# Every fifth chunk of layer 1's weighting goes from DVE to ACT

## The chip, the cores and the metric

The kernel runs on one core of a Trainium2 chip. The time is device microseconds of the whole kernel. Beside the unprofiled runs there is one profiled execution, with a trace of every instruction; its own time and its span (first to last instruction in the trace) are given below. Engines are called PE (matmul), DVE (vector), ACT (scalar), POOL (GpSimd, which issues the gathers) and SP (which issues the plain DMAs).

## The reference, cut to what matters

Two graph-attention layers on 2048 nodes with 256 features, 8 batches, one sparse adjacency shared by all (the probability of an edge is 2 x 0.0039, and every node is its own neighbour). Each layer is followed by a residual and a layer norm. Layer 1, where the change is:

```python
q = (h @ W).reshape(B, N, H, D)                 # H = 4 heads, D = 64
e_src = jnp.einsum('bnhd,d->bnh', q, a_src)
e_dst = jnp.einsum('bnhd,d->bnh', q, a_dst)
e = e_src[:, :, None, :] + e_dst[:, None, :, :]
e = jnp.where(e >= 0, e, 0.2 * e)
e = jnp.where(mask, e, NEG_INF)                 # mask: the adjacency
attn = jax.nn.softmax(e, axis=2)
h_prime = jnp.einsum('bijh,bjhd->bihd', attn, q)
y = layernorm(x + elu(h_prime))
```

Only neighbours count: for node i, head h and batch b the kernel sums attn x q over the 12 to 38 neighbours of i and no others.

## The kernel before, in words

**Tiling.** The nodes are sorted by degree and cut into 16 tiles of 128. Tile t has room for K = `SLOTS[t]` neighbours (38, 24, 23, 21, 20, 19, 19, 18, 17, 17, 16, 15, 15, 14, 13, 12). The batches are taken in two halves of four. One unit of work is (layer, half h, tile t), so each layer has 32 units. In layer 1 the tiles of half 0 run from t = 15 down to 8, then 0, then 7 to 1; those of half 1 in the reverse of that order, so the last unit of all is t = 15 with K = 12.

**A unit of layer 1.** POOL gathers, slot by slot, the k-th neighbour's row of 128 nodes with an indirect DMA (L189: 128 rows, each with 4 batches of 256 features and 4 logit terms). Two slots make a chunk (`CHUNK`), which fills one tile of a ring of 16 (`RING`); a chunk's ring tile is free again when PE has summed it. K = 38 is done in two parts of 19 slots, all others in one.

- `logits1`: DVE adds the node's own term to each chunk's logit terms (L744, one per chunk), then leaky ReLU, mask and softmax over the K slots (L752 to L759, exp on ACT at L760, sum and reciprocal L766 and L768). `pw = p / sum` goes into a PSUM tile (L769); `p` itself stays in SBUF, without the division. For K = 38 `pw` is the copy of `p` without division (L771), and the two parts are combined later.
- `sums1`: per chunk DVE multiplies the rows in place by `pw`, one weight for each slot, batch, head and its 64 columns (L793, 2048 columns for two slots, 1024 for the last chunk of an odd K). PE then adds each slot into PSUM by products with the identity (L609, four of 64x64 per slot, into two `acc` tiles per part; there are four such tiles in all).
- `after1`: for K = 38 the two parts are scaled and added (`shares`, L813, L819). Then ELU and residual (ACT L824, L825 give `ex`; DVE L829, L832), statistics (DVE L370, L371), `z` (ACT L381, L382), `rstd` and `nmr` (DVE L383 to L389), normalising on ACT (L393), and four scatters of the result by POOL (L197).

**What sets the order.** A generator scheduler written in the kernel (`tick`) emits the instructions: the sums of one unit are interleaved with the logits of the units ahead and the `after1` of the unit before. POOL's queue runs in exactly that order (`manual_schedule` for Pool). The instructions of the other engines are placed by the framework's own scheduler, so their order in the built program isn't always the emitted one. Credits on the ring (`pump`) let a gather be emitted only when a tile is due to come free.

In layer 0 the logits are dot products on DVE (L540), and the weighting there is done on ACT already, 256 columns at a time (L631).

Of the kernel before, what the change touches and what calls it, by code (L numbers as in the profile page):

```python
# [16 lines left out]
AF = mybir.ActivationFunctionType  # L17
ALU = mybir.AluOpType
# [4 lines left out]
P = 128  # L23
ALPHA = 0.2
EPS = 1e-5
H = 4
D = 64
# [10 lines left out]
CHUNK = 2  # L38
RING = 16
LEAD = 5  # L40
LATE = 6

FAR = float(2**16)

# [79 lines left out]
def fast_path(  # L124
# [24 lines left out]
    nc = tc.nc  # L149
# [3 lines left out]
    HB = B // 2  # L153
    HC = HB * C
    HG = HB * H
# [19 lines left out]
    def ps_tile(name):  # L175
        return ps.tile([P, 512], F32, tag="ps", name=name)

    def acc_tile(name):
        return psa.tile([P, 512], F32, tag="acc", name=name)
# [66 lines left out]
    for it in range(NT):  # L246
        v = adjs[it][:, :N]
# [30 lines left out]
    for it in range(NT):  # L278
# [6 lines left out]
        i = it // 2  # L285
# [138 lines left out]
    class Unit:  # L424
        def __init__(self, layer, h, t):
            self.layer, self.h, self.t = layer, h, t
            self.K = SLOTS[t]
            self.name = f"{layer}_{h}_{t}"

            n = self.K if self.K <= RING * CHUNK * 3 // 4 else -(-self.K // 2)  # L430
            self.parts = [(k, min(n, self.K - k)) for k in range(0, self.K, n)]
            self.chunks = [[] for _ in self.parts]
            self.p = [None] * len(self.parts)

            self.m, self.s = [], []
            self.ready = False
# [166 lines left out]
    def add_slot(u, acc, k, K, rows, s):  # L603

        w_ = (C, CD)[u.layer]
        for c in range(2):
            for r in range(2):
                rr = slice(64 * r, 64 * r + 64)
                nc.tensor.matmul(  # L609
                    acc[r][64 * c : 64 * c + 64, :],  # L610
                    lhsT=ident[rr, rr],
                    rhs=rows[rr, s, c * 2 * w_ : (c + 1) * 2 * w_].rearrange(
                        "p (j w) -> p j w", j=2
                    )[:, :, :C],
                    start=(k == 0),
                    stop=(k == K - 1),
                    tile_position=(64 * r, 64 * c),
                )
# [110 lines left out]
    def logits1(u):  # L729

        while not u.ready:
            yield 0
        for i, (k0, K) in enumerate(u.parts):
            n, o = f"{u.name}_{i}", offs[u.t] + k0
            wide = [P, K, HG]
            so = u.own.rearrange("p (b g) -> p b g", b=HB)
            e = ep.tile(wide, F32, tag="e", name=f"e_{n}")
            for c in range(-(-K // CHUNK)):
                while len(u.chunks[i]) <= c:
                    yield 0  # L740
                while clock[0] < u.chunks[i][c][2] + 5:
                    yield 0
                rows, ns, _ = u.chunks[i][c]
                nc.vector.tensor_tensor(  # L744
                    e[:, c * CHUNK : c * CHUNK + ns, :].rearrange("p s (b g) -> p s b g", b=HB),
                    rows[:, :ns, :].rearrange("p s (b w) -> p s b w", b=HB)[:, :, :, C:],
                    so.unsqueeze(1).to_broadcast([P, ns, HB, H]),
                    ALU.add,
                )
                yield ns  # L750
            p = e
            nc.vector.scalar_tensor_tensor(p, e, ALPHA, e, ALU.mult, ALU.max)  # L752
            nc.vector.tensor_tensor(
                p, p, neg[:, o : o + K].unsqueeze(2).to_broadcast(wide), ALU.add
            )
            yield 0
            m = sp.tile([P, HG], F32, tag="m1", name=f"m1_{n}")
            nc.vector.tensor_reduce(m, p.rearrange("p k c -> p c k"), AX.X, ALU.max)
            nc.vector.tensor_tensor(p, p, m.unsqueeze(1).to_broadcast(wide), ALU.subtract)  # L759
            nc.scalar.activation(p, p, AF.Exp)  # L760
            yield 0
            yield 0

            pw = ps_tile(f"p_{n}")[:, : K * HG].rearrange("p (k c) -> p k c", k=K)
            sm = sp.tile([P, HG], F32, tag="s1", name=f"s1_{n}")
            nc.vector.tensor_reduce(sm, p.rearrange("p k c -> p c k"), AX.X, ALU.add)  # L766
            if len(u.parts) == 1:
                nc.vector.reciprocal(sm, sm)  # L768
                nc.vector.tensor_tensor(pw, p, sm.unsqueeze(1).to_broadcast(wide), ALU.mult)  # L769
            else:  # L770
                nc.vector.tensor_copy(pw, p)  # L771
            u.m.append(m)
            u.s.append(sm)
            u.p[i] = pw
            yield 0

    def sums1(u):
        u.xr = xrp.tile([P, 2, HW], F32, tag="xr", name=f"xr_{u.name}")
        nc.sync.dma_start(u.xr.rearrange("p r c -> p (r c)"), x1s[u.h][ts(u.t, P), :])
        while evictions:  # L780
            evictions.popleft()()
        u.accs = []
        for i, (k0, K) in enumerate(u.parts):
            while u.p[i] is None:
                yield 0
            acc = [acc_tile(f"acc_{u.name}_{i}_{r}") for r in range(2)]
            for c in range(-(-K // CHUNK)):
                rows, n, _ = u.chunks[i][c]
                v = rows[:, :n, :].rearrange("p s (b w) -> p (s b) w", b=HB)
                v = v[:, :, :C].rearrange("p a (g d) -> p a g d", d=D)  # L790
                pv = u.p[i][:, c * CHUNK : c * CHUNK + n, :]
                pv = pv.rearrange("p k (b g) -> p (k b) g", b=HB)
                nc.vector.tensor_tensor(  # L793
                    v, v, pv.unsqueeze(3).to_broadcast([P, n * HB, H, D]), ALU.mult
                )
                for s in range(n):
                    add_slot(u, acc, c * CHUNK + s, K, rows, s)
                    if s == n - 1:
                        credits[0] += 1
                    yield 1  # L800
            u.accs.append(acc)

    def after1(u):
# [35 lines left out]
        def store(o):  # L839
            for r in range(2):  # L840
                for j in range(2):
                    scatter(
                        "out",
                        out.rearrange("b n c -> (b n) c"),
                        oidx[:, h, j, t, r : r + 1],
                        o[:, 2 * r + j, :],
                    )
# [8 lines left out]

        late.append((clock[0] + LATE, lambda: store(o)))

# [21 lines left out]
    for j, u in enumerate(units):  # L880
        u.index = j
    before = (before0, before1)
    logits = (logits0, logits1)
    sums = (sums0, sums1)
    after = (after0, after1)
    ahead = [0.0]
# [32 lines left out]
    for j, u in enumerate(units):  # L919
# [5 lines left out]
        if 2 <= j < 10:  # L925
            b, half = divmod(j - 2, 2)
            n = ts(half, N // 2)
            nc.sync.dma_start(xg[1][n, ts(b, C)], x[HB + b, n])
        left = float(u.K)
        for share in sums[u.layer](u):  # L930
# [3 lines left out]
            if not begun and left <= u.K / 2 and j + 3 < len(units):  # L934
                begun = True
                v = units[j + 3]
# [302 lines left out]
```

## Time and profile before

| | us |
|---|---|
| median of three runs (2752.2 to 2755.29) | 2752.31 |
| profiled execution, its own time | 2757.27 |
| its span | 2755.5 |
| DVE busy, whole span | 2358.9 |
| ACT busy, whole span | 1475.2 |
| PE busy, whole span | 1884.3 |
| POOL busy, whole span | 1509.5 |

The stretch from 1767 to 2690 us, which is layer 1 from near its beginning to its last gather, by busy time of each engine (923 us): DVE 874.55, POOL 681.91, PE 598.60, ACT 148.64; the DMA engines are busy 0.89 of it at 325 GB/s.

In the profile's rows a group is a line of the kernel, its engine and operation, what it writes and reads (out<-in), and the number of instructions; then busy time, mean of one in ns, and the idle time of the engine just ahead of them with what ended it. "<-issue" stands for idle time that no wait in the trace explains. In the 40 slices a digit is the busy share in tenths; one slice is 68.9 us. The line numbers are those of the kernel before.

### The profile page before, as it was taken

The numbers are of one execution on the slowest core, as the hardware profiler recorded it, in microseconds if no ns is written. First come the engines' busy times: TensorE is split into PE (matmuls) and PEld (weight loads), VectorE is DVE, ScalarE is ACT, GpSimd is POOL, SyncE is SP. The second block draws the span as 40 slices with busy tenths as digits, with TensorE's granted clock in tenths as the row PEclk, the third lists the DMA queues.
The fourth block names the chain that finished last, engine by engine and source line by source line (L and its number), as shares of the span: only waits on it lengthen the run. The fifth ranks groups of instructions, "written<-read, shape, count | busy, mean of one in ns | idle before, by whom it ended". The sixth has DMA issues, their size and how long they took to land. (4 is left out here: it accounts for less than half of the span.)

```text
span 2755.5 us, 41008 instructions
## 1 busy us (share of the span) xinstructions
PE 1884.3 (68%) x12003; PEld 788.4 (29%) x12003; DVE 2358.9 (86%) x7255; ACT 1475.2 (54%) x3465; POOL 1509.5 (55%) x1506
## 2 busy tenths in 40 slices
PE   0148888888776767676878677766566576675663
PEld 0123434333333334343333322311122112121221
DVE  7679999999987875777787786799999899999996
ACT  6137777878779986868788779221111111210212
POOL 1354454545444543544544455577767777775772
PEclk9569899999898888898888888878878888877886
DMA  9996776868674665767776765799789999986991
GB/s 388 386 374 216 263 278 226 281 227 274 233 244 168 212 218 197 262 215 254 234 263 229 257 223 193 272 337 351 270 313 352 329 335 335 361 312 254 340 337 66
DMA packets 248024, 749.41 MB, mean 272 GB/s; under 512 B 55712, under 2 KB 73248, under 8 KB 241648
## 3 DMA queue, kind: packets, MB, share of 16 engines
q0 software_dynamic: 192064, 644.32, 66.2%
q1 hardware_dynamic: 54464, 101.21, 10.3%
q8 instruction: 98, 1.61, 0.2%
q10 hardware_dynamic: 1264, 1.18, 0.1%
q14 instruction: 134, 1.10, 0.1%
HBM read 721.50 MB, written 84.48 MB: 292 GB/s over the span
## 5 line engine op out<-in xcount | busy, mean ns | idle before, releaser
L609 PE MATMUL acc<-s,ident 64*64 64x512 f32 x9632 | 1363.4, 659 | 448.5 <-issue 226.6
L540 DVE CUSTOM_DVE_ANT_0 j<-s,g 128x256 bf16<-128x256 f32 x2408 | 1019.5, 423 | 201.5 <-DMA s<-xg,idx 135.9
L189 POOL DMA_INDIRECT s<-xg,idx x602 | 631.0, 1048 | 769.0 <-ACT s L631 283.5
L631 ACT ACTIVATE s<-s,e 128x256 f32<-128x256 f32 x2408 | 999.2, 503 | 27.3 <-DVE e L566 26.5
L189 POOL DMA_INDIRECT s<-qg,idx x602 | 610.6, 1014 | 249.9 <-issue 123.8
L609 PEld LDWEIGHTS acc<-s,ident 64*64 64x64 f32 x9632 | 386.5, 145 | 1219.2 <-issue 675.6
L793 DVE TENSOR_TENSOR s<-s,p 128x2048 f32<-128x2048 f32 (+1 forms) x312 | 682.0, 2201 | 0.8 <-issue 0.2
L381 ACT ACTIVATE z<-mv,roots 128x4 f32<-128x4 f32 x64 | 18.9, 296 | 509.7 <-DVE mv L371 509.6
L540 DVE DVE_READ_ACCUMULATOR2_ANT e<- 128x1 f32 x2408 | 196.0, 81 | 0.0
L693 PE MATMUL ps_q<-wqs,x1T 128*128 128x264 f32 x512 | 147.4, 425 | 37.2 <-ACT x1T L405 25.9
L197 POOL DMA_INDIRECT out_dram<-o,oidx x128 | 129.9, 1015 | 75.2 <-ACT o L393 40.1
L403 PE MATMUL ps_t_x<-ident,xo 128*128 128x128 f32 x256 | 56.6, 364 | 165.1 <-DMA xo<-xg,order 165.1
L393 ACT ACTIVATE o<-xr,nmr,rstd 128x256 f32<-128x256 f32 x128 | 66.4, 589 | 134.1 <-DVE nmr L389 102.2
L413 PE MATMUL ps_p_g<-A,xT 128*128 128x256 f32 x512 | 129.8, 400 | 9.5 <-DVE so L702 5.5
L413 PE MATMUL ps_p_h<-w_sb,hT 128*128 128x256 f32 x512 | 127.8, 392 | 1.5 <-ACT hT L405 1.5
L693 PEld LDWEIGHTS ps_q<-wqs,x1T 128*128 128x128 f32 x512 | 100.5, 206 | 88.9 <-ACT x1T L405 31.2
L413 PEld LDWEIGHTS ps_p_g<-A,xT 128*128 128x128 f32 x512 | 97.1, 197 | 53.8 <-DVE so L702 9.0
L488 DVE MAX8 m<-nb 128x8 f32<-128x2048 f32 x44 | 100.5, 2285 | 13.3 <-DMA nb<-edges,order 13.2
L413 PEld LDWEIGHTS ps_p_h<-w_sb,hT 128*128 128x128 f32 x512 | 92.1, 190 | 63.3 <-issue 19.5
L760 ACT ACTIVATE e<-e 128x304 f32<-128x304 f32 (+11 forms) x34 | 14.9, 439 | 175.7 <-DVE e L759 175.6
L403 PEld LDWEIGHTS ps_t_x<-ident,xo 128*128 128x128 f32 x256 | 37.9, 184 | 232.9 <-issue 219.0
L393 ACT ACTIVATE y<-y,nmr,rstd 128x256 f32<-128x256 f32 x128 | 67.2, 589 | 32.1 <-DVE nmr L389 31.8
(128 smaller groups left out, 1426.6 us busy)
## 6 DMA issues: line engine op xcount, KB each, us to landing
adj<-in_adj_dram SPq DMA_DIRECT2D x16, 1024.0 KB, 8.9
edges<-adj SPq DMA_DIRECT2D x16, 1024.0 KB, 19.7
xr<-xo SPq DMA_DIRECT2D x128, 128.0 KB, 6.7
x1s<-y SPq DMA_DIRECT2D x32, 512.0 KB, 7.4
xr<-x1s SPq DMA_DIRECT2D x32, 512.0 KB, 6.9
s<-xg,idx POOLq DMA_INDIRECT x602
s<-qg,idx POOLq DMA_INDIRECT x602
xg<-in_x_dram SPq DMA_DIRECT2D x4, 2048.0 KB
```

Source lines behind the costliest of these rows:

```text
L189: nc.gpsimd.indirect_dma_start(out=dst, out_offset=None, in_=table, in_offset=AT(ap=index, axis=0), bounds_check=table.shape[0] - 1, oob_i ...
L197: ins = nc.gpsimd.indirect_dma_start(out=table, out_offset=AT(ap=index, axis=0), in_=src, in_offset=None)
L381: nc.scalar.activation(z, mv[:, :, 1], AF.Ln, bias=w.roots[:, 0:1])
L393: nc.scalar.activation(dst[:, b, :], y[:, b, :], AF.Identity, bias=nmr[:, b : b + 1], scale=rstd[:, b : b + 1],)
L403: nc.tensor.transpose(pt[:, ts(j, P)], src[:, ts(4 * i + j, P)], ident)
L413: nc.tensor.matmul(pp[:, ts(j, C)], lhsT=srcT[:, ts((2 * i + j) * KC + k, P)], rhs=weight[:, k, :], start=(k == 0), stop=(k == KC - 1),)
L488: nc.vector.max(m[:, ts(i, 8)], v)
L540: nc.vector.tensor_tensor_reduce(out=jt, in0=rows[:, s, ts(b, C)], in1=u.g[:, ts(b, C)], scale=1.0, scalar=0.0, op0=ALU.mult, op1=ALU.add, ...
L609: nc.tensor.matmul(acc[r][64 * c : 64 * c + 64, :], lhsT=ident[rr, rr], rhs=rows[rr, s, c * 2 * w_ : (c + 1) * 2 * w_].rearrange("p (j w) ...
L631: nc.scalar.activation(v, v, AF.Copy, scale=u.p[i][:, b, k : k + 1])
L693: nc.tensor.matmul(pq[:, : C + 2 * H], lhsT=x1T[:, ts(i * KC + k, P)], rhs=w.wqs[:, k, :], start=(k == 0), stop=(k == KC - 1),)
L793: nc.vector.tensor_tensor(v, v, pv.unsqueeze(3).to_broadcast([P, n * HB, H, D]), ALU.mult)
```

## The change

A constant `SHARE = 5` is added. In `sums1`, the chunks 4, 9, ... of each part (every fifth) are multiplied by ACT and not by DVE: one activation (Copy with a per-partition scale) for each slot, batch and head, 64 columns each, so 32 for a chunk of two slots and 16 for one of one slot. They are emitted at the first chunk of each group of five, ahead of DVE's multiplication of that chunk, if the fifth chunk exists. ACT reads its weights from `p` in SBUF, not from `pw` in PSUM. For units of one part the columns of `p` that belong to these chunks are therefore divided by the sum as well, in place, by one small DVE instruction for each such chunk (after L769). For K = 38 `p` is used as it stands.

In the changed kernel later lines carry other numbers: L744 becomes L747, the small multiplication is L777, ACT's is L809, DVE's L793 becomes L813; PE's L609 becomes L612, and L813, L824, L829 become L840, L851, L856.

```diff
+SHARE = 5
...
             self.p = [None] * len(self.parts)
+            self.ps = [None] * len(self.parts)
...
             if len(u.parts) == 1:
                 nc.vector.reciprocal(sm, sm)
                 nc.vector.tensor_tensor(pw, p, sm.unsqueeze(1).to_broadcast(wide), ALU.mult)
+
+                for k in range((SHARE - 1) * CHUNK, K, SHARE * CHUNK):
+                    own = p[:, k : min(k + CHUNK, K), :]
+                    some = [P, own.shape[1], HG]
+                    nc.vector.tensor_tensor(own, own, sm.unsqueeze(1).to_broadcast(some), ALU.mult)
             else:
                 nc.vector.tensor_copy(pw, p)
             u.m.append(m)
             u.s.append(sm)
-            u.p[i] = pw
+            u.p[i], u.ps[i] = pw, p
             yield 0
...
-            for c in range(-(-K // CHUNK)):
+            chunks = -(-K // CHUNK)
+
+            def weighted(c):
                 rows, n, _ = u.chunks[i][c]
                 v = rows[:, :n, :].rearrange("p s (b w) -> p (s b) w", b=HB)
                 v = v[:, :, :C].rearrange("p a (g d) -> p a g d", d=D)
-                pv = u.p[i][:, c * CHUNK : c * CHUNK + n, :]
+                pv = (u.ps if c % SHARE == SHARE - 1 else u.p)[i]
+                pv = pv[:, c * CHUNK : c * CHUNK + n, :]
                 pv = pv.rearrange("p k (b g) -> p (k b) g", b=HB)
-                nc.vector.tensor_tensor(
-                    v, v, pv.unsqueeze(3).to_broadcast([P, n * HB, H, D]), ALU.mult
-                )
+                if c % SHARE == SHARE - 1:
+                    for a in range(n * HB):
+                        for g in range(H):
+                            nc.scalar.activation(
+                                v[:, a, g, :], v[:, a, g, :], AF.Copy, scale=pv[:, a, g : g + 1]
+                            )
+                else:
+                    nc.vector.tensor_tensor(
+                        v, v, pv.unsqueeze(3).to_broadcast([P, n * HB, H, D]), ALU.mult
+                    )
+
+            for c in range(chunks):
+                if c % SHARE == 0 and c + SHARE - 1 < chunks:
+                    weighted(c + SHARE - 1)
+                if c % SHARE != SHARE - 1:
+                    weighted(c)
+                rows, n, _ = u.chunks[i][c]
                 for s in range(n):
                     add_slot(u, acc, c * CHUNK + s, K, rows, s)
```

## The prediction

> **What bounds the kernel now.** I read, in this order: the page's busy shares and 40 slices, the costliest groups, the waits of POOL after 1800 us, and the timelines of POOL, DVE, PE and ACT where those waits are long.
>
> ```profile
> DVE  7679999999987875777787786799999899999996
> ACT  6137777878779986868788779221111111210212
> POOL 1354454545444543544544455577767777775772
> DMA  9996776868674665767776765799789999986991
> L189 POOL DMA_INDIRECT s<-qg,idx x602 | 610.6, 1014 | 249.9 <-issue 123.8 <-PE acc L609 73.5 <-DMA s<-qg,idx 11.9
> L793 DVE TENSOR_TENSOR s<-s,p 128x2048 f32<-128x2048 f32 (+1 forms) x312 | 682.0, 2201 | 0.8 <-issue 0.2
> ```
>
> Layer 1 is the last 14 slices or so. DVE is at 9 tenths there, ACT at 1 or 2, and POOL shows 7. A reader stops at DVE, and L793 (682 us) is the very work that the change cuts. But POOL's 7 is a full queue. Its waits from 1800 us on:
>
> ```profile
> POOL s L189 <- issue: 111.9, 367, 0.3
> POOL s L189 <- PE acc L609: 49.3, 43, 16.0
> POOL out_dram L197 <- ACT o L393: 40.1, 13, 19.6
> ```
>
> The 367 waits for "issue" are all 0.3 us: a pause that follows every gather, however busy POOL is. So one gather costs 0.99 + 0.30 = 1.29 us of POOL's time. I went through POOL's timeline: between 1766.60, after the last long wait at the seam of the layers, and 2689.07, the last gather, it starts 673 DMAs in 922.5 us, and only 36.2 us of that is waiting beyond the usual pause. All of it is for ring space, in three places:
>
> ```profile
> 2013.38 0.99 POOL L189 DMA_INDIRECT s<-qg,idx  x1 [9.80 <-PE acc L609]
> 2547.65 1.45 POOL L189 DMA_INDIRECT s<-qg,idx  x1 [16.05 <-PE acc L609]
> 2689.07 0.99 POOL L189 DMA_INDIRECT s<-qg,idx  x1 [0.30 <-issue]
> ```
>
> These are 9.5 us, 15.7 us, and between them 11.0 us in nine short waits from 2180 to 2305. With no wait at all the stretch would take 886.3 us (1.319 a DMA, as some take longer). POOL is a bound right behind DVE.
>
> Second reading: how long before its use by L744 was a chunk's last gather issued? Pairing both in order, DVE was made to wait for data at 1725.09 (gather at 1719.20: 5.9 us) and 2195.73 (gather at 2189.02: 6.7 us). About 6 us is thus the least possible. Up to unit (0,1) and on to 2342 nearly every unit's last chunk is used 4 to 7 us after its issue (two at 9): DVE already runs as fast as POOL feeds it. Only from 2345 does it fall behind, to about 11 us; at the end the last gather waits 12.1 us:
>
> ```profile
> 2701.14 0.19 DVE L744 TENSOR_TENSOR e<-s,own 128x32 f32<-128x32 f32 x1
> ```
>
> Third reading, the two long POOL waits. Both follow a unit of K=38, which holds all four `acc` tiles:
>
> ```profile
> 2543.04 17.75 PE L609 MATMUL acc<-s,ident 64*64 64x512 f32 x136 [20.10 <-issue]
> 2542.25 1.89 DVE L813 TENSOR_TENSOR v<-acc,fs 128x512 f32<-128x512 f32 x3
> ```
>
> PE stands 20.1 us until L813 frees a tile, and DVE's queue has L813 behind seven L793 of the next unit.
>
> **What the Trainium skill says.** "ScalarE: Activation LUTs", section on what ACT_TABLE_LOAD costs: an ACTIVATE takes 186 ns + 0.833 ns per element, a pointer operand adds about 93, back-to-back ones overlap by about 93. The trace agrees: L631 (256 columns, one pointer) takes 503 ns, predicted 492, and four in a row take
>
> ```profile
> 1005.60 1.71 ACT L631 ACTIVATE s<-s,e 128x256 f32<-128x256 f32 x4
> ```
>
> so each further one adds (1.71 - 0.51)/3 = 0.40 us. "VectorE: DVE Perf Modes", TRN2 errata: fp32 tensor_tensor is (N+151)/0.96 ns, 2.29 us at 2048; the trace has 2.28. "DMA: Bandwidth & Descriptors", SWDGE vs HWDGE vs iDMA: GpSimd computes the descriptors of these DMAs in software; the trace's steady 0.99 us for a 128-row gather fits. No page says how the two engines slow each other on one ring tile; no run here shows it for this shape.
>
> **The change, part by part.** Per half of the batch 25 chunks go to ACT: 21 of two slots and 4 of one. In all 42 and 8, or 42x32 + 8x16 = 1472 ACT instructions, which is what the changed kernel's order holds.
>
> Removed from DVE: of two L793 in a row, 4.48 us, the second adds 2.20; a half chunk adds 1.13 (3.41 for one of each). 42x2.20 + 8x1.13 = 101.4 us.
>
> Added to DVE: 42 multiplications of a chunk's own weights by 1/sum (128x32; L744 of that shape takes 0.18 us, 0.10 to 0.18 in sequence): 42x0.15 = 6 us. They stand ahead of the unit's first L793, so they lie on the path. Net 95 us less on DVE.
>
> Added to ACT, an operation the trace lacks (64 columns): low 0.40 - 192x0.00084 = 0.24 us a step, from L631; the skill's figures, 186+53+93-93, give an estimate of the same. High 0.34, if nothing overlaps. I take 0.24: 7.7 us a full block, 353 us in all (500 at the high end). Layer 1 leaves ACT some 40 of each 50 us.
>
> Order on ACT: a block starts once its unit's own weights are there, as DVE starts L793. PE takes chunks in order; DVE reaches the fifth place after 4x2.2 + 2x0.1 = 9.0 us, the block is ready at 7.7, so PE does not wait. Behind the block ACT holds `ex` (L824, L825) of the unit before, which DVE needs at L829. In the changed kernel's order DVE comes to L829 after six to eight L793, 13 us or more, for K up to 19 and after K=38 (in the last unit, K=12, after two, and there `ex` is slipped into the block after its first step); ACT has it at 7.7 + 2.3 = 10. For K=20 to 24 DVE comes after five or six L793, 12 us, and ACT, with one step of the second block slipped in, has it at 10.1. `z` stands behind the second block (17.5 us) and is asked for at about 21. At 0.24 nothing waits; at 0.34 the K=20 to 24 units wait 1 to 3 us each.
>
> POOL and PE keep their order of instructions; no DMA is added or moved but that five pairs of SP's small loads and stores change places.
>
> Now where the 95 us go. POOL's 673 DMAs stay, so DVE's time counts only where it keeps POOL waiting, and after the last gather:
>
> 1. Seam (to 1766): DVE waits there for gathers and for layer 0's last unit. 0 us; 2 either way.
> 2. K=38, 2013: one L793 fewer ahead of L813, 2.2 - 0.15 = 2.05 gained. 7.4 us of wait stay.
> 3. 2180 to 2305, K=24, 23: the waits for the ring of a unit's first chunk (1.35, 1.33, 1.11) stay: no chunk before it left. The other six wait for the fifth to eighth chunk, now earlier: 9.95 less six pauses, 8.1 gained.
> 4. K=38, 2547: 2.05 again. Also DVE no longer lags: last chunk 6 us after issue and not 9.6, so POOL is 3.6 us less ahead. 5.7 gained, 10 stay.
> 5. The end: the last gather is used after 6.3 us and not 12.1: 5.8.
> 6. The last unit: five L793 and not six, 2.05.
>
> Sum 2.05 + 8.1 + 5.7 + 5.8 + 2.05 = 23.7 us. Span 2755.5 - 23.7 = 2731.8; profiled execution 2757.27 - 23.7 = 2733.6. It stands 5 us above the median of 2752.31, so the median is predicted at 2728.6. The other 71 us become waits of DVE for gathers.
>
> **Rivals.** (a) POOL never waits: all 36.2 us, with 5 and 6 44 us, 2708. For it: DVE has 71 us to spare. Against: the `acc` tiles stay four, and L813 keeps its place but for one L793. (b) DVE's gain in full, 2657: against it stands POOL's floor of 886 us and a DMA share already of 0.93 to 0.98 in many 50 us windows; only a cheaper gather would give it. (c) Half the gain: ACT steps of about 0.34 make DVE wait at L829 or for `z` in the ten or so K=19 to 24 units, some 12 us: 2740. (d) No change: the K=38 and K=24 waits are a round trip (gather, logits, softmax, first product, PE) that no engine's rate shortens; only 5 or 6 would be left, 2750. (e) Slower: ACT's queue. If a step costs over about 0.5 us (two SBUF-bound engines in each other's way), a block takes 16 us and `ex` comes at 18, when DVE stands at L829 in the middle units too; each further 0.1 us a step holds DVE and PE 3 us in each of 30 units. At 0.62, about 110 us of waits against the 95 taken from DVE: some 15 us slower, 2767. Against it: L631 keeps its 0.40 us step beside a busy DVE.
>
> **How the numbers follow.** Forecast case 0.60 (2718 to 2738), (a) 0.12, (b) 0.02, (c) 0.09, (d) 0.09, (e) 0.08. About 0.2% (5.5 us) is what a measurement of this kernel can tell from no change. Faster 0.83, same 0.09, slower 0.08. The range leaves out (b), (e) and most of (d): 2706 to 2747.
>
> **What would show it.** L809 groups at about 340 ns each and steps of 0.24; DVE's busy sum down by about 95 us, with its waits for `s<-qg` up from 34 us to 80 or more; POOL's waits for `PE acc` after 1800 down to 25 to 35 us, with the two long ones still there, near 7 and 10; last use 6 us after the last gather. Wrong would be: DVE waiting much for ACT (`ex`, `z`, `e`) - then (c) or (e); the two long waits gone - then (a); a gather's 0.99 us changed - then my floor is none.

## The result, and the profile after

The changed kernel takes 2741.39 us (median of five runs, 2740.53 to 2743.51). The kernel before took 2755.29 us beside it; the ratio of the two is 0.995, with a 95% interval of 0.9939 to 0.9961. The forecast was 2728.6 with a range of 2706 to 2747: the direction and the range held, the gain was smaller. The profiled execution went from 2757.27 to 2741.96 us (15.3 less), its span from 2755.5 to 2740.1.

The page's 40 slices of the changed kernel:

```profile
DVE  7679999999987876777787786788888888888996
ACT  6137787878879986867878779644445555554454
POOL 1353454545444544544454545577767777777773
DMA  9996776777765566767686774899789998997892
```

DVE fell from 9 to 8 in layer 1 and ACT rose from 1 or 2 to 4 or 5. POOL's row hardly moved. The multiplications were handed over as forecast; from the costliest groups:

```profile
L813 DVE TENSOR_TENSOR s<-s,p 128x2048 f32<-128x2048 f32 (+1 forms) x262 | 577.5, 2222 | 0.0
L809 ACT ACTIVATE s<-s,e 128x64 f32<-128x64 f32 x1472 | 357.8, 335 | 47.1 <-DVE e L777 35.8
L191 POOL DMA_INDIRECT s<-qg,idx x602 | 614.8, 1021 | 233.4 <-issue 123.7
```

L813 (L793 before) is 50 instructions and 104.5 us lighter. ACT's new group has 1472 instructions of 335 ns. Back to back they start 0.239 us apart (median in the trace), so a full block takes 7.7 us:

```profile
2234.86 7.75 ACT L809 ACTIVATE s<-s,e 128x64 f32<-128x64 f32 x32 [2.10 <-DVE e L777]
```

That is the low end of the forecast's bounds and the value which it took, measured beside a busy DVE. DVE's busy sum over the whole span is 2270.1 us and was 2358.9, so 88.8 less. The gathers' mean went from 1014 to 1021 ns, which the forecast had not foreseen.

Where did the 88.8 us go? What DVE waited for between 1767 and 2690 us in the changed kernel:

```profile
DVE e L747 <- DMA s<-qg,idx: 84.1, 62, 4.1
DVE s L769 <- ACT e L763: 12.9, 26, 0.6
DVE rstd L385 <- ACT z L384: 8.1, 12, 0.7
DVE e L747 <- issue: 5.3, 3, 4.4
DVE xr L856 <- ACT ex L852: 0.6, 1, 0.6
```

The first row in the kernel before, in the same window:

```profile
DVE e L744 <- DMA s<-qg,idx: 24.4, 20, 5.8
```

So 60 us of the relief became waiting for gathered rows. The waits for ACT (21.6 us together) were 15.8 before: ACT's new work is not what DVE waits for.

I account for the rest by POOL's queue; that it sets the pace is what the experiments test. Its stretch from the last long wait at the seam to the last gather is the same 672 steps in both kernels:

| | before | after |
|---|---|---|
| end of the seam's wait | 1766.60 | 1764.45 |
| last gather | 2689.07 | 2681.49 |
| the stretch | 922.5 | 917.0 |
| of it, POOL busy | 681.0 | 686.0 |
| of it, waits beyond the 0.3 us pause | 36.2 | 25.9 |
| last gather to the end of the span | 66.4 | 58.6 |

So the span's 15.4 us are 2.1 at the seam, 5.4 in the stretch and 7.8 behind the last gather. The waits left in the stretch, from POOL's timeline of the changed kernel:

```profile
2010.82 0.99 POOL L191 DMA_INDIRECT s<-qg,idx  x1 [9.03 <-PE acc L612]
...
2264.39 1.03 POOL L199 DMA_INDIRECT out_dram<-o,oidx  x1 [2.95 <-ACT o L395]
...
2302.54 1.03 POOL L199 DMA_INDIRECT out_dram<-o,oidx  x1 [1.72 <-ACT o L395]
...
2539.29 1.45 POOL L191 DMA_INDIRECT s<-qg,idx  x1 [10.35 <-PE acc L612]
```

The two waits for the `acc` tiles after K = 38 are still there. The nine short waits for ring space between 2180 and 2305 have shrunk to two (1.87 and 1.78 us), but in their place stand two that weren't there: a scatter of the finished unit waits for `o`. The cause is seen on DVE just ahead of the first of them:

```profile
2254.11 2.27 DVE L813 TENSOR_TENSOR s<-s,p 128x2048 f32<-128x2048 f32 x1
2256.31 0.15 DVE L385 TENSOR_TENSOR rstd<-z 128x4 f32<-128x4 f32 x1
...
2256.48 2.28 DVE L813 TENSOR_TENSOR s<-s,p 128x2048 f32<-128x2048 f32 x1
2258.68 0.15 DVE L386 SCALAR_TENSOR_TENSOR rstd<-mv,rstd 128x4 f32<-128x4 f32 x1
...
2258.75 2.28 DVE L813 TENSOR_TENSOR s<-s,p 128x2048 f32<-128x2048 f32 x1
2260.95 0.15 DVE L387 SCALAR_TENSOR_TENSOR rstd<-rstd,z 128x4 f32<-128x4 f32 x1
...
2261.12 2.28 DVE L813 TENSOR_TENSOR s<-s,p 128x2048 f32<-128x2048 f32 x1
2263.32 0.15 DVE L391 SCALAR_TENSOR_TENSOR nmr<-mv,rstd 128x4 f32<-128x4 f32 x1
```

Four instructions of 0.15 us, each behind a multiplication of the next unit: `z` is there at 2254.78, `nmr` starts 8.5 us later, ACT normalises at 2263.51, and POOL, which no longer waits for ring space here, stands at the scatter. In the kernel before DVE's order was the same, but POOL came to the scatter later, at 2268.03, and stood no longer than its usual pause.

### The profile page after: what moved, and what is told of

It reads as the page before. It is cut to its first block, busy times and chain, and to the rows that moved or that the text cites. A ratio compares the mean times of both kernels' runs of the same rounds, so it can differ in the third digit from the quotient of the medians.

```text
span 2740.1 us, 42566 instructions
## 1 busy us (share of the span) xinstructions
PE 1857.8 (68%) x12003; PEld 792.3 (29%) x12003; DVE 2270.1 (83%) x7247; ACT 1827.9 (67%) x4937; POOL 1515.4 (55%) x1506
## 3 DMA queue, kind: packets, MB, share of 16 engines
q1 hardware_dynamic: 54464, 101.21, 10.4%
## 5 line engine op out<-in xcount | busy, mean ns | idle before, releaser
L612 PE MATMUL acc<-s,ident 64*64 64x512 f32 x9632 | 1336.4, 653 | 469.0 <-issue 285.4
L191 POOL DMA_INDIRECT s<-qg,idx x602 | 614.8, 1021 | 233.4 <-issue 123.7
L612 PEld LDWEIGHTS acc<-s,ident 64*64 64x64 f32 x9632 | 391.1, 144 | 1211.5 <-issue 777.6
L813 DVE TENSOR_TENSOR s<-s,p 128x2048 f32<-128x2048 f32 (+1 forms) x262 | 577.5, 2222 | 0.0
L809 ACT ACTIVATE s<-s,e 128x64 f32<-128x64 f32 x1472 | 357.8, 335 | 47.1 <-DVE e L777 35.8
L747 DVE TENSOR_TENSOR e<-s,own 128x32 f32<-128x32 f32 (+1 forms) x312 | 56.9, 186 | 104.0 <-DMA s<-qg,idx 97.6
## 6 DMA issues: line engine op xcount, KB each, us to landing
edges<-adj SPq DMA_DIRECT2D x16, 1024.0 KB, 19.8
```

Source lines behind the costliest of these rows:

```text
L191: nc.gpsimd.indirect_dma_start(out=dst, out_offset=None, in_=table, in_offset=AT(ap=index, axis=0), bounds_check=table.shape[0] - 1, oob_i ...
L612: nc.tensor.matmul(acc[r][64 * c : 64 * c + 64, :], lhsT=ident[rr, rr], rhs=rows[rr, s, c * 2 * w_ : (c + 1) * 2 * w_].rearrange("p (j w) ...
L747: nc.vector.tensor_tensor(e[:, c * CHUNK : c * CHUNK + ns, :].rearrange("p s (b g) -> p s b g", b=HB), rows[:, :ns, :].rearrange("p s (b w ...
L809: nc.scalar.activation(v[:, a, g, :], v[:, a, g, :], AF.Copy, scale=pv[:, a, g : g + 1])
L813: nc.vector.tensor_tensor(v, v, pv.unsqueeze(3).to_broadcast([P, n * HB, H, D]), ALU.mult)
```

## The experiments

Theory A: POOL's issuing of gathers and scatters sets the pace of layer 1; DVE's relief counts only where it shortens a wait of POOL, and behind the last gather. Rival B: ACT's blocks take part of the gain. Rival C: the bytes of the gathers (the DMA engines) set the pace, so POOL's issuing doesn't matter.

The runs came in three groups, each with the kernel before beside it. The first group fell on a chip where the kernel before takes 2864.08 us; in the second and third it takes 2758.33 and 2756.65. Ratios are to the kernel before of the same group. The times expected for group 1 were made for a chip on which the kernel before takes 2755 us; all four came out longer, and only differences inside the group count.

| run | edit, in short | us | ratio (95% interval) |
|---|---|---|---|
| group 1 | before: 2864.08 | | |
| no_weight | fifth chunks not weighted | 2855.94 | 0.998 (0.9966 to 0.9995) |
| plain_before | before, plain output stores by SP, rows left in sorted order | 2773.64 | 0.968 (0.9658 to 0.9702) |
| plain_after | changed, plain output stores | 2732.14 | 0.9539 (0.9522 to 0.9556) |
| evict_after | changed, `acc` tiles freed early | 2849.03 | 0.9949 (0.9932 to 0.9966) |
| group 2 | before: 2758.33 | | |
| after_again | changed | 2743.77 | 0.9946 (0.9926 to 0.9966) |
| evict_before | before, `acc` tiles freed early | 2748.74 | 0.9966 (0.9951 to 0.9981) |
| late_after | changed, scatters later | 2736.86 | 0.9934 (0.9916 to 0.9952) |
| evict_late_after | changed, both | 2725.61 | 0.9883 (0.9864 to 0.9902) |
| group 3 | before: 2756.65 | | |
| no_weight_2 | as no_weight | 2739.12 | 0.9941 (0.9926 to 0.9956) |
| plain_before_2 | as plain_before | 2746.25 | 0.9959 (0.9945 to 0.9974) |
| plain_after_2 | as plain_after | 2675.44 | 0.9702 (0.9688 to 0.9716) |
| share4_after | changed, `SHARE` 4 | 2736.91 | 0.9927 (0.9909 to 0.9945) |

### Is ACT's new work in anybody's way?

```diff
                 if c % SHARE == SHARE - 1:
-                    for a in range(n * HB):
-                        for g in range(H):
-                            nc.scalar.activation(
-                                v[:, a, g, :], v[:, a, g, :], AF.Copy, scale=pv[:, a, g : g + 1]
-                            )
+                    pass
```

> The changed kernel, but the fifth chunks are multiplied by nothing at all: ACT's 1472 instructions are left out, and with them the weighting of those chunks. DVE's, PE's and POOL's work is that of the changed kernel. Theory A (POOL's gathers and their round trips set the time, ACT's blocks hold nobody): 2737 to 2743 us, no more than 4 us from the changed kernel's 2741.4, with a mean gather back from 1.021 to about 1.014 us at most. Rival B (ACT's blocks eat part of DVE's 95 us: PE waits for them, or `ex`, `z` and the exp stand behind them): 2733 us or less, with DVE's waits for ACT (21.6 us between 1767 and 2690) down by the same amount.

> The changed kernel as it stands, beside the others of this call. Theory A (POOL's issuing is the bound): its gain over the kernel before is some 14 us on the first chip. On the second chip, where POOL also pauses after every 6 gathers or so, the kernel without the fifth chunk's weighting gained 8 us, and the changed kernel then gains 4 to 10 (ratio 0.9965 to 0.9985). Rival B (ACT's blocks cost something): on that chip no gain or a loss, ratio 0.999 or more, while leaving the blocks out gave 0.998.

> As the first run without the fifth chunk's weighting (ACT's 1472 instructions left out, and with them that part of the computation), to be compared with the changed kernel on the first kind of chip (0.9946 to 0.995 of the kernel before, POOL's DMAs 1.020 us each, 54 of them over 1.05 us after 1767). Theory A: ratio 0.992 to 0.996, so ACT's blocks cost nothing on the path. If ACT's blocks cause POOL's longer DMAs: 42 long ones again, a mean of 1.014, and 3 to 5 us less time, ratio 0.993. Rival B (DVE and PE wait for ACT): 0.990 or less.

In group 1 the kernel without ACT's blocks gained only 0.2% on the kernel before. That group holds no run of the changed kernel, and POOL behaves otherwise on that chip. From POOL's waits after 1800 us there:

```profile
POOL s L191 <- issue: 132.8, 419, 3.6
POOL s L191 <- remote: 102.8, 62, 2.8
POOL s L191 <- PE acc L612: 34.9, 21, 7.7
```

"remote" is a release that the profile could not tie to an engine of this core; the kernels on the first chip show none. In the timeline POOL issues 5 to 14 gathers at the usual pace and then mostly stands 1.2 to 2.5 us. Group 3 is again on a chip like the first: 0.9941 without the blocks, against 0.9946 and 0.995 with them. Taking all of ACT's 357.8 us away gives 1 to 3 us by these ratios, and the intervals overlap, so no cost of the blocks is shown. DVE's waits stay too: 85.6 us for `s<-qg` (84.1 with the blocks) and the same 21.6 us for ACT. Rival B is out: its number was 0.990 or less. POOL's longer gathers are mostly still there without the blocks: 49 DMAs over 1.05 us after 1767, against 54 in the changed kernel and 42 before. If the blocks caused them, 42 were expected. The count moves by itself as well: late_after and share4_after, which have the blocks, show 48 and 47. What these DMAs have in common stands at the end.

### What is DVE's relief worth when POOL has time?

```diff
             for r in range(2):
-                for j in range(2):
-                    scatter(
-                        "out",
-                        out.rearrange("b n c -> (b n) c"),
-                        oidx[:, h, j, t, r : r + 1],
-                        o[:, 2 * r + j, :],
-                    )
+                for c in range(2):
+                    b0, n0 = h * HB + 2 * c, t * P + 64 * r
+                    nc.sync.dma_start(
+                        out[b0 : b0 + 2, n0 : n0 + 64, :].rearrange("j n c -> n j c"),
+                        o[64 * c : 64 * c + 64, 2 * r : 2 * r + 2, :],
+                    )
```

> The kernel before, with the 128 scatters of the output on POOL replaced by plain DMAs on SP of the same bytes in the sorted order of the nodes (the rows are not put back in their places). POOL has 112 DMAs of 1.3 us, 146 us, less to issue in the stretch of 923 us. Theory A: DVE (874 us busy of 923) becomes the bound, so 25 to 45 us are gained there and some 5 at the end: 2705 to 2730 us. Rival C (the bytes of the gathers or the DMA engines set the time, not POOL's issuing): within 8 us of 2755.

> The changed kernel with the same replacement. Theory A: with POOL out of the way DVE's 72 us less count, so the change is worth 50 to 75 us here and not 14: 2640 to 2670 us. Rival C: within 8 us of 2741, the change worth 14 again. Rival D (PE or the chain from a gather to its sum limits both): in between, 2690 to 2720, the change worth 15 to 25.

> The kernel before, its output written by SP's plain DMAs in sorted order (rows not put back), on a chip where the kernel before takes about 2755. On the other chip this took 90 us off, but there POOL had pauses of its own. Theory A: with POOL out of the way DVE (874 us of the 923) is the bound, 2705 to 2730 us (ratio 0.981 to 0.991). Rival C (bytes, not issuing): 0.997 or more.

> The changed kernel with the same replacement. Theory A: DVE's 72 us less now count for the most part, the change is worth 35 to 70 us here (ratio 0.958 to 0.976), where it is worth 14 with POOL's scatters in place. Rival C: 0.992 to 0.997. If PE or the round trip of the ring is the next bound: the change is worth 15 to 30.

This pair of runs decides. In group 3 the replacement alone is worth 10.4 us (2756.65 to 2746.25), less than the 25 to 50 expected, and this run alone would hardly tell theory A from rival C (its interval reaches 0.9974, rival C began at 0.997). The traces show where the rest went. POOL now runs ahead and waits for ring space:

```profile
POOL s L189 <- PE acc L609: 197.9, 89, 16.9
```

Its stretch fell from 922.5 to 902.8 us, 861.5 of it DVE work, but the time behind the last gather rose from 66.4 to 74.2. DVE was closer behind POOL than I had put it. But with it in place the change is worth 2746.25 - 2675.44 = 70.8 us, five times the 14 us that it is worth with the scatters on POOL. The same rows of 1 KB are written and the same gathers made; what differs is who issues the stores, through which DMA queue, and where the rows go. That the scatters held up gathers in their common queue doesn't show: where DVE waits for a gathered row, the wait ends in the median 6.3 us after the gather's issue in the changed kernel and 6.5 us in plain_after_2. In plain_after_2 the row of DVE's waits for gathers and that of POOL's waits are:

```profile
DVE e L747 <- DMA s<-qg,idx: 31.2, 22, 3.6
```

```profile
POOL s L191 <- PE acc L612: 118.1, 68, 13.8
POOL s L191 <- issue: 115.1, 369, 2.2
```

Now POOL waits for ring space (118.1 us, in the changed kernel 31.6) and DVE for gathers 31.2 us (84.1 there). POOL's stretch takes 841 us, with 779.7 us of DVE work in it. The DMA engines reach a share of 0.94 and 355 GB/s there, where the changed kernel has 0.89 and 327: the bytes were not at their limit, and rival C is out for this chip. In group 1 the change is worth 41.5 us with plain stores (50 to 75 expected); what it is worth there without them was not measured.

### Do the `acc` tiles hold POOL after K = 38, and the scatters at K = 23 and 21?

```diff
+            if len(u.parts) == 2 and i == 0:
+                kept = wide_tile(f"k_{u.name}")[:, :HC]
+                kept = [kept[:, ts(r, HW)] for r in range(2)]
+                for r in range(2):
+                    nc.scalar.copy(kept[r], acc[r])
+                acc = kept
             u.accs.append(acc)
```

```diff
-LATE = 6
+LATE = 9
```

> The changed kernel, and ACT copies the two `acc` tiles of the first part of K=38 to SBUF when they are done, so that the next unit has two free tiles and its sums need not wait until the parts are combined. Theory A with my reading of POOL's two long waits (8.7 and 10.0 us beyond the pause, after K=38, held by the `acc` tiles): both go or fall under 3 us, 2722 to 2730 us. If these waits are the round trip of the ring itself (the rest of rival A of the prediction not being there): within 4 us of 2741.

> The kernel before, with the first part of K=38 copied out of its `acc` tiles by ACT when it is done, DVE keeping all of its multiplications. If POOL's waits alone set the time: the two waits after K=38 (9.5 and 15.7 us on the first chip) go, 20 to 25 us. If DVE is a bound right beside POOL: half of that or less, 5 to 14 us (ratio 0.995 to 0.998), since DVE is 5 to 10 us behind the gathers there. Rival (the wait is not the `acc` tiles): nothing, within 3 us.

> The changed kernel with `LATE` 9 and not 6: POOL's scatters of a unit stand some 3 gathers later in its queue. In the changed kernel POOL now waits 2.65 and 1.42 us for `o` in the units of K=23 and 21 (at 2264 and 2302 us), and the gathers behind these scatters reach DVE late (4.4 us at 2276). If these waits ate part of the gain: 2 to 6 us faster than the changed kernel. If not, or if the scatters held no one: within 2 us.

> The changed kernel with both: the `acc` tiles of K=38's first part copied out early, and `LATE` 9. Theory A: 12 to 19 us for the two waits after K=38 and 2 to 6 for the scatters, 14 to 24 us below the changed kernel on the first chip (2717 to 2727 us), less on the second, where POOL's own pauses are the larger part. Rival (the round trip of the ring holds POOL at these places whatever frees the tiles): no more than 6 us below.

evict_after fell into group 1 and settles little: no run of the changed kernel stands beside it there, and POOL's other pauses there are larger than the waits in question. In group 2, `LATE` 9 takes 6.9 us off the changed kernel (2743.77 to 2736.86). The intervals of the two ratios overlap, so this gain is likely and not shown; the two waits were 4.1 us. Both waits for `o` are gone from POOL's timeline. Freeing the tiles early takes a further 11.3 us, and here the intervals stand apart. The whole is 2725.61 us, 18.2 below the changed kernel beside it and 32.7 below the kernel before, and the fastest of the versions that leave nothing out. In the place of the two long waits POOL's timeline of this version has, later in the same units:

```profile
2026.13 0.99 POOL L191 DMA_INDIRECT s<-qg,idx  x1 [2.92 <-PE acc L612]
...
2545.73 0.99 POOL L191 DMA_INDIRECT s<-qg,idx  x1 [6.01 <-PE acc L612]
```

9.03 and 10.35 became 2.92 and 6.01: the tiles did hold POOL, and behind them stands the next limit, further down the ring, whose cause was not looked for. On the kernel before the same edit is worth 9.6 us of the 25 that POOL waited there: with DVE close behind, the rest turned into other short waits (`o` again, 16.1 us in 20 waits).

### More of the same

```diff
-SHARE = 5
+SHARE = 4
```

> The changed kernel with `SHARE` 4 and not 5: every fourth chunk goes to ACT (17 more blocks of two slots or so in all, another 35 us off DVE). Theory A: POOL sets the pace, so it is worth nothing: within 4 us of the changed kernel, ratio 0.993 to 0.997, DVE's waits for gathers up by 20 us or more. Rival E (DVE's load still counts in full or by half): 10 us or more below the changed kernel, ratio 0.991 or less. If ACT's queue is near its limit (two blocks of 7.7 us ahead of `ex` and `z` in the small units): slower than the changed kernel by 5 us or more.

DVE's work between 1767 and 2690 us falls by another 30 us (802.4 to 772.2), and the time by 4.5 to 7 us (2736.91 against 2741.39 and 2743.77). From DVE's waits:

```profile
DVE e L747 <- DMA s<-qg,idx: 101.6, 70, 3.9
...
DVE xr L856 <- ACT ex L852: 11.1, 7, 3.5
```

17.5 us more waiting for gathers (20 or more were expected), and 10.5 us more for `ex`, which ACT has behind its blocks. The ratio 0.9927 lies just outside the 0.993 to 0.997 expected and the gain just above the 4 us allowed; its interval and the changed kernel's overlap, so a small gain is likely and left open. Rival E (10 us or more below the changed kernel, 0.991 or less) is not met, though the interval just reaches 0.991.

## Why the prediction was right or wrong, step by step

**What bounds the kernel: right.** POOL's issuing sets the pace of layer 1; plain_before_2 and plain_after_2 show it (the change is worth 14 us with the scatters on POOL, 70.8 without). One reading was too narrow: the "about 6 us" from a gather to its first use is a middle value. Over the 18 waits of DVE for gathers after 1767 in the kernel before, it was 5.2 to 8.9 us. That DVE's relief would turn into waits for gathers was right in kind and near in size: 60 us more, where 71 were forecast.

**ACT's price and order: right.** 335 ns and 0.239 us a step, 7.7 us a block. DVE waits 0.6 us for `ex` and 8.1 us for `z` in all, and just as much with the blocks left out. The estimate of 0.24 us a step, worked out from the Trainium skill, "ScalarE: Activation LUTs", section on what ACT_TABLE_LOAD costs, agrees with the trace's 0.239 us for an operation that the kernel before does not have.

**Step 1, the seam: 0 forecast, 2.1 in the two profiles.** This may be chance: over the profiles of these chips without the remote waits the seam's last wait ends anywhere from 1762.1 to 1768.3, with the kernel before at 1766.60.

**Step 2, K = 38 at 2013: wrong, 2.05 forecast and 0.8 measured.** The step that failed is "one L793 fewer ahead of L813". The order is not the old one with a gap. Between the end of the softmax and the combination DVE has six multiplications in both kernels: the scheduler put another chunk into the place of the one that left. First multiplication to combination is 13.70 us before (1994.76 to 2008.46) and 13.69 after (1992.02 to 2005.71).

**Step 3, the short waits at 2180 to 2305: wrong in size, 8.1 forecast and 3.9 measured.** The ring waits did go (11.0 us beyond the pause to 3.1, so 7.9). What failed is that the step asked only for waits that go, and not for what POOL would reach next: it reached two scatters before `o` was ready, 2.65 and 1.42 us early. In late_after, with the scatters moved, both waits are gone. Steps of this size are not exact: in the second profile of the changed kernel (after_again) waits beyond the pause between 2160 and 2305 sum to 9.1 us, where the first has 7.1, again with two of these scatters waiting for `o` and a third at 2225.

**Step 4, K = 38 at 2547: right, 5.7 forecast and 5.7 measured.** Here the order did lose one multiplication, seven before and six after, and DVE no longer lagged.

**Steps 5 and 6, the end: right, 7.85 forecast and 7.8 measured.** The last gather at 2681.49 is used at 2687.56, 6.07 us later and not 12.06:

```profile
2687.56 0.19 DVE L747 TENSOR_TENSOR e<-s,own 128x32 f32<-128x32 f32 x1
```

**Not in the sum: POOL's DMAs took 5.0 us more** for the same 672 (681.0 to 686.0). The median gather is 0.99 us in both; it is the long ones, over 1.05 us, which are 54 and were 42. The profiles without weighting and with plain stores (561 DMAs there and not some 687) have 49 and 51. The forecast's "flat-out" 886.3 us was thus no constant. The last section shows where the long ones fall.

The sum of what was measured: 2.1 + 0.8 + 3.9 + 5.7 + 7.8 - 5.0 = 15.3, against the forecast's 23.7. The median missed by 12.8 us: 8.4 are this sum, and 4.4 that the profiled execution stood 5.0 us above the median before and only 0.6 after. The forecast had carried the 5.0 over; beside the changed kernel, the kernel before had a median of 2755.29 us, so 3.0 of it was a base put too low from three runs. The range held because it was wide: the gain was 11 to 14 us, by which median of the kernel before one takes, and not 23.7.

**The rivals.** (a), POOL never waits, did not come: evict_late_after, which goes that way, shows that it takes two further edits. (b) needs POOL's scatters out of the way, and then 70.8 of the 95 us come. (c) gave the closest time (2740), but for a reason that the runs exclude: ACT's steps took 0.239 us and not 0.34, and DVE does not wait longer for ACT with them than without. (d) was right in one point, that waits of a round trip stay when an engine gets lighter. (e) did not come near.

## What to carry to other kernels

Where a queue with many short equal pauses feeds the busiest engine, sum that queue from its first item to its last before counting on the busy engine: what an edit is worth is the fall of its waits, and the tail behind its last item. After each wait that is taken away, ask what the queue reaches next and whether that is ready: here it was the output of the unit before, and moving its scatters three gathers back took those waits away. With an order made by a scheduler, count the instructions in the new order at each place that the sum uses; "one fewer" may be filled up.

## What the runs showed that was not expected

POOL's long DMAs fall on certain instructions of DVE. All 54 in the changed kernel after 1767 us, and all 42 in the kernel before, overlap a DVE instruction with two inputs in SBUF: the residual L856, the additions and multiplications of the softmax, L747, or the combination of the two parts. Of all 687 DMAs there, 341 overlap one, and of the other 346 none is long. One long one, and what DVE ran beside it:

```profile
2101.85 2.07 POOL L191 DMA_INDIRECT s<-qg,idx  x1 [0.31 <-issue]
2101.83 1.22 DVE L856 TENSOR_TENSOR xr<-xr,ex 128x1024 f32<-128x1024 f32 x1
```

50 of the 54 end 0.83 to 0.89 us after the end of such an instruction, and each of the 25 DMAs that start in an L856 with more than 0.2 us of it left is long. Of the 258 that overlap none of these and start during an L813, whose weights lie in PSUM, none takes more than 1.04 us. Beyond 0.99 us each, the long ones cost 14.7 us of POOL's stretch in the kernel before and 19.8 in the changed one: these are the 5.0 us. More of them met such an instruction, and met it earlier in its run; the forecast had no term for that. No run changed where these operands lie, so the link is read from traces and not tested.

One chip stood apart in POOL. On it the kernel before took 2864 us and not 2755, and POOL mostly stood 1.2 to 2.5 us after every 5 to 14 gathers, 102.8 us in one run, with a release that the profile ties to no engine of this core. Replacing the scatters was worth 90 us there and 10 us on the chip of group 3. The cause was not tested, nor whether it belongs to the chip or to the moment.

A scalar instruction of 64 columns in place, with its scale from a pointer, has a step of 0.239 us while DVE multiplies another tile of the same ring (0.238 us in the 57 steps in which DVE stood idle). DVE's multiplications hardly changed either: the mean of all L813 rose from 2201 to 2222 ns because fewer of them are short. At equal shape it stayed:

```profile
L793 DVE TENSOR_TENSOR s<-s,p 128x2048 f32<-128x2048 f32 x290 | 655.6, 2276 | 0.8 <-issue 0.2
L813 DVE TENSOR_TENSOR s<-s,p 128x2048 f32<-128x2048 f32 x248 | 560.6, 2279 | 0.0
```
